# The inverse roots of the first token tiles: one VectorE step and GpSimd's power in place of ScalarE's root and VectorE's Newton steps

## The chip, the core and the metric

The kernel runs on one core of a Trainium2 chip. A core has five engines that run side by side and wait for each other through semaphores: TensorE (PE in the profile, with its weight loads shown as PEld), VectorE (DVE), ScalarE (ACT), GpSimd (POOL) and SyncE (SP), which here only issues DMA transfers. Each engine takes its own instructions strictly in the order in which they were written. Matmul results land in PSUM, everything else lives in SBUF.

The metric is the device time of one execution in microseconds (us). Smaller is better.

## The reference, cut to what matters

The input `x` holds 4 sequences of 1024 tokens with 512 features, that is, 4096 rows. `cond` has one row of 128 numbers per sequence.

```python
scale = cond @ norm_w.T + 1.0                        # one factor per sequence and feature
ms = jnp.mean(x * x, axis=-1, keepdims=True)         # one number per token
h = x * (scale[:, None, :] * jax.lax.rsqrt(ms + EPS))
u = h @ up_w.T                                       # 512 -> 4096
val, gate = jnp.split(u, 2, axis=-1)
h = val * jax.nn.gelu(gate, approximate=False)
hq = act_quant(h)                                    # 8 bits per token
wq = weight_quant(down_w)                            # -1, 0, 1
y = hq @ wq.T                                        # 2048 -> 512
return y + x
```

The change touches `rsqrt(ms + EPS)` alone, and that only for the first 512 tokens. For each token it is one number.

## The kernel before, in words

The kernel takes the four sequences one after the other. For a sequence it computes the up projection in 16 groups of columns, with gate and value beside each other, quantizes the result and multiplies it by the rounded down weights. From the second sequence on, the up and down products of neighbouring sequences are interleaved, and TensorE is never short of work. The first sequence has to begin from nothing. This beginning, the head, is what the change touches: about the first 20 us.

The order of the work is written out by hand (`tc.manual_schedule()`): every engine receives its instructions in the order of the Python text, so whatever stands ahead in an engine's queue is done first.

The head does this for the first 512 tokens, the tiles n = 0 to 3 of 128 tokens each:

- SyncE asks for tiles 0 and 1 in one transfer, 2 and 3 in a second, then for the first rows of the up weights, and so on. ScalarE's queue brings the row of `cond`.
- TensorE multiplies dummy tiles (`keep_warm`, L967) while it waits for data. These dummies stand in its queue like any other work: 4 of them ahead of the small matmul `pd` (L236), and 7 between `pd` and the first transposes.
- `first_sum` (L918) sums the squares of a tile: tiles 0 and 2 on ScalarE, 1 and 3 on VectorE. The sums go to the columns of `ssq0`.
- `rsqrt_root` (L925) lets ScalarE take the square root of two columns, and `rsqrt_steps` (L931) lets VectorE take the reciprocal of it and one Newton step: five short VectorE instructions. The result goes to two columns of `rs0`. This is done once for tiles 0 and 1, once for tiles 2 and 3.
- `cond_range_steps` (L214) makes the factor `dg` of the first sequence in four short VectorE instructions. The small matmul `pd`, and so all 7 dummies after it, wait for `dg`. In the kernel before, these four are interleaved with the first Newton steps by `in_turn` (L305). In the same way `w_factor_steps` (L293), the factor of the first weight tile (three instructions), is interleaved with the second Newton steps.
- `first_scale` (L945) multiplies a tile by its inverse roots: tiles 0, 1 and 2 on ScalarE, tile 3 on VectorE.
- `first_turn` (L952) transposes the scaled tile on TensorE, four 128x128 blocks per tile, into four PSUM banks `ptx`. Bank k holds block k of all four tiles. The tiles are turned in the order 0, 1, 3, 2. After them come the four transposes `pw` of the first weight tile (`w_turn`, L339), which GpSimd has scaled (`w_scale`, L331).
- `first_high` (L959, ScalarE) and `first_low` (L963, VectorE) split each bank into two 16-bit parts, `w_high` (L363) and `w_low` (L372) do it for the weights, and `plain_first` (L644) multiplies them. From there on TensorE is almost never idle.

Later tiles have their own way: `rsqrt` (L488 to L491) with one VectorE or GpSimd step for the mean and one GpSimd instruction `pow` with the exponents from `neghalf`. Tiles 4 to 7 go through it in `second_part` (L1040).

ScalarE works with a table of functions that is loaded by an instruction of its own. The kernel before loads the one with the square root at L904, while it waits for data, and the one with the nonlinearity (Gelu) at L1042, in the middle of `second_part`. Squares and copies run under either table.

GpSimd begins with two instructions MODIFY_POOL_CONFIG, which stand ahead of its first piece of work and name the code that it is to run. It meets such a pair again further on, where it changes between elementwise work and the maximum over partitions.

Of the kernel before, what the change touches and what calls it, by code (L numbers as in the profile page):

```python
# [2 lines left out]

# [6 lines left out]
F32 = mybir.dt.float32  # L10
# [4 lines left out]
AF = mybir.ActivationFunctionType  # L15
# [4 lines left out]
P = 128  # L20
# [31 lines left out]
def glu_quant_kernel(  # L52
# [158 lines left out]
        PE.transpose(pm, mx, ident)  # L211
        return pm

    def cond_range_steps(pm, b0, b1):  # L214
        n = b1 - b0
        dg = sm.tile([B, B], F32, name=f"dg_{b0}", tag="dg")[:n, :n]
        yield dg
        d4 = sm.tile([B, 1], F32, name=f"d4_{b0}", tag="d4")[:n]
        DVE.tensor_reduce(d4, pm, AX.X, ALU.max)
        yield  # L220
        DVE.tensor_scalar(d4, d4, 1e-30, None, ALU.max)
        yield
        pow2_floor(d4)
        yield
        DVE.tensor_scalar(dg, ident[:n, :n], d4, 1.0 / X_UP, ALU.mult, ALU.mult)

    def cond_range(pm, b0, b1):
        steps = cond_range_steps(pm, b0, b1)
        dg = next(steps)
        in_turn(steps)  # L230
        return dg

    def cond_spread(dg, b0, b1, tag):
# [53 lines left out]
    def w_largest(j, t0=0, t1=2):  # L287
        t = slice(t0, t1)
        am = sm.tile([P, 2], F32, name=f"wam_{j}_{t0}", tag="wam")[:, t]
        DVE.tensor_reduce(am, wn(j)[:, t], AX.X, ALU.max, apply_absolute_value=True)  # L290
        return am

    def w_factor_steps(j, am, t0=0, t1=2):  # L293
        t = slice(t0, t1)
        pow2_floor(am)
        yield
        DVE.scalar_tensor_tensor(
            sw[:, j, t], am, 2.0**-100, undo_up[:, t], ALU.max, ALU.mult
        )
        yield  # L300
        if j not in iv:
            iv[j] = sm.tile([P, 2], F32, name=f"iv_{j}", tag="iv", bufs=3)
        DVE.reciprocal(iv[j][:, t], sw[:, j, t])

    def in_turn(*steps):  # L305

        for _ in zip_longest(*steps):
            pass

    def w_factor(j, am, t0=0, t1=2):  # L310
        in_turn(w_factor_steps(j, am, t0, t1))

    def w_range(j, t0=0, t1=2):
        w_factor(j, w_largest(j, t0, t1), t0, t1)
# [582 lines left out]

    ctx.enter_context(tc.manual_schedule())
    start_t = sm.tile([P, 1], F32, name="start_t", bufs=1)
    eps = sm.tile([P, 1], F32, name="eps", bufs=1)  # L900
    DVE.memset(eps, EPS)
    ACT.dma_start(out=cn, in_=cond[0:1])
    SP.dma_start(out=nw, in_=norm_w.rearrange("(k p) c -> p k c", p=P))
    ACT.activation(start_t, one, AF.Sqrt)  # L904


    X0 = H[:, 4:8].rearrange("p s h d -> p (s h) d")
# [10 lines left out]
    def first_sum(n, eng=ACT):  # L918
        v, j, a = X0[:, n], junk[:, n % 4], ssq0[:, n : n + 1]
        if eng is ACT:  # L920
            ACT.activation(j, v, AF.Square, accum_out=a)
        else:
            eng.scalar_tensor_tensor(j, v, 1.0, v, ALU.mult, ALU.mult, accum_out=a)

    def rsqrt_root(n, m):  # L925

        z = sm.tile([P, m], F32, name=f"newton_{n}", bufs=1)
        ACT.activation(z, ssq0[:, n : n + m], AF.Sqrt, scale=1.0 / D, bias=eps)
        return z

    def rsqrt_steps(n, m, z):  # L931

        t, y = ssq0[:, n : n + m], rs0[:, n : n + m]
        ms = sm.tile([P, m], F32, name=f"mean_sq_{n}", bufs=1)
        DVE.reciprocal(y, z)
        yield
        DVE.tensor_scalar(ms, t, 1.0 / D, EPS, ALU.mult, ALU.add)
        yield
        DVE.tensor_tensor(z, y, y, ALU.mult)
        yield  # L940
        DVE.scalar_tensor_tensor(z, z, -0.5, ms, ALU.mult, ALU.mult)
        yield
        DVE.scalar_tensor_tensor(y, z, 1.5, y, ALU.add, ALU.mult)

    def first_scale(n, eng):  # L945
        r = rs0[:, n : n + 1]
        if eng is ACT:
            ACT.activation(X0[:, n], X0[:, n], AF.Copy, scale=r)
        else:
            eng.tensor_scalar(X0[:, n], X0[:, n], r, 1.0, ALU.mult, ALU.mult)  # L950
# [34 lines left out]
    pm = cond_over(mx, 0, 1, "A")  # L985
    first_sum(0)
    first_sum(1, DVE)
    root = rsqrt_root(0, 2)
    keep_warm(4)
    steps = cond_range_steps(pm, 0, 1)  # L990
    dg = next(steps)
    next(steps)
    next(steps)
    in_turn(rsqrt_steps(0, 2, root), steps)
    pd = cond_spread(dg, 0, 1, "A")
    keep_warm(7)
    first_sum(2)
    first_sum(3, DVE)
    am = w_largest(0, 1, 2)
    root = rsqrt_root(2, 2)  # L1000
    factor = w_factor_steps(0, am, 1, 2)
    in_turn(rsqrt_steps(2, 2, root), islice(factor, 2))
    first_scale(0, ACT)
    first_scale(1, ACT)
    in_turn(factor)
    first_scale(3, DVE)
    first_scale(2, ACT)
    w_scale(0, (1,))
    cond_undo(pd, 0, 1)
    ptx = [po_bank(f"ptx_0_{k}") for k in range(3)] + [bank("A", 2, name="ptx_0_3")]  # L1010
    for n in (0, 1, 3, 2):
        first_turn(n, ptx)
    w_turn(0, [bank("E", 2, name=f"pw_0_{t}") for t in (1, 0)], (1,))
    w_range(0, 0, 1)
# [16 lines left out]
    def second_part():  # L1031
        w_turn(0, ts=(0,))
        w_high(0, (0,))
        w_low(0, (0,))
        w_scale(1, (1,))
        first_sum(6)
        first_sum(7)
        first_low(0, 1, ptx[1])
        first_low(0, 2, ptx[2])
        rsqrt(ssq0[:, 4:8], rs0[:, 4:8], DVE)  # L1040
        first_low(0, 3, ptx[3])
        ACT.activation(start_t, neghalf[:, 0:1], AF.Gelu)  # L1042

# [546 lines left out]
```

## Time and profile before

| quantity | value |
|---|---|
| median of 3 runs | 727.5 us (727.32, 727.5, 730.2) |
| the profiled execution's own time | 727.02 us |
| its span in the profile | 725.2 us, so 1.8 us lie around it |
| TensorE busy | 718.7 us, 99% of the span |
| VectorE, ScalarE, GpSimd busy | 583.2, 396.4 and 195.9 us |
| ScalarE's table loads | L904 at 1.29 us, L1042 at 17.46 us, 1.28 us each |
| first work of GpSimd after four memsets | 10.59 us (L331) |

In a line of a timeline the first number is the start in us from the span's beginning, the second the duration; then come the engine, the line of the kernel, the operation, what is written and read with the shapes, and how many instructions were merged into the line. A bracket names the idle time of the engine just before and what ended it. In a chain of waits each line gives the start, the share of time and who held the end up in it. The chain for the whole span is 97% TensorE, so the time is the sum of what TensorE does and of the few places where it waits; nearly all of the latter lie in the head.

### The profile page before, as it was taken

Reading aid. Unit: us, or ns where it says so; the run is one execution under the profiler, and the core shown is the slowest. Engines: PE = TensorE matmul, PEld = TensorE weight load, DVE = VectorE, ACT = ScalarE, POOL = GpSimd, SP = SyncE. Lnnn points to the kernel's source line nnn. Section 1 sums busy time; section 2 is a strip of 40 time slices with the busy share of each in tenths; the row PEclk is TensorE's granted clock in tenths of the full one; section 3 lists DMA queues with packets and bytes.
Section 4 is the critical chain, followed back from the end, with each engine's and each line's share of the span. In section 5 each row is a group of like instructions: output and inputs, shape, how many; then the busy total and the mean of one; then the engine's idle time right before and its main releaser. Section 6 shows DMA issues by size and latency. Waiting matters only on the chain.

```text
span 725.2 us, 10130 instructions
## 1 busy us (share of the span) xinstructions
PE 718.7 (99%) x3656; PEld 358.4 (49%) x3656; DVE 583.2 (80%) x824; ACT 396.4 (55%) x622; POOL 195.9 (27%) x205
## 2 busy tenths in 40 slices
PE   8999999999999999999999999999999999999998
PEld 4544444444444446665444445665444444445844
DVE  8977887985698899787689897687678888755897
ACT  6769866772337674554335676544433665332274
POOL 1578796775100033340000030360020000000100
DMA  9399999989544565867745646766955455443253
GB/s 322 103 310 276 295 264 254 279 172 225 117 103 102 132 144 141 206 164 169 176 101 103 131 101 183 192 160 160 202 118 102 102 102 102 102 101 89 95 183 116
DMA packets 224062, 117.83 MB, mean 162 GB/s; under 512 B 186358, under 2 KB 196743, under 8 KB 224012
## 3 DMA queue, kind: packets, MB, share of 16 engines
q1 hardware_dynamic: 223722, 116.86, 65.7%
q8 instruction: 28, 0.46, 0.3%
q10 hardware_dynamic: 290, 0.33, 0.1%
q14 instruction: 22, 0.18, 0.1%
HBM read 49.50 MB, written 23.09 MB: 100 GB/s over the span
## 4 chain that ended last, share of the span: by engine, by line
PE 97%; DMA 2%; ACT 0%; DVE 0%; issue 0%; SPq 0%; ACTq 0%
PE A L586 34%; PE E L586 17%; PE pg L601 11%; PE pv L601 10%; PE B L586 9%; PE po L854 8%; PE po_end L806 4%; DMA SXY<-H 1%; PE po L806 1%; DMA H<-in_x_dram 1%; PE ptx L955 1%; PE pv L644 0%; PE po_B L854 0%; PE pg L644 0%; PE pw L339 0%; PE po_E L854 0%
## 5 line engine op out<-in xcount | busy, mean ns | idle before, releaser
L586 PEld LDWEIGHTS <-SXY 128*128 128x128 f16 x2016 | 197.2, 98 | 232.3 <-issue 0.6
L586 PE MATMUL A<-R,SXY 128*128 128x512 f16 x1152 | 266.3, 379 | 0.0
L586 PE MATMUL E<-R,SXY 128*128 128x512 f16 x576 | 140.0, 379 | 0.1
L684 DVE SCALAR_TENSOR_TENSOR H<-A,sg,t 128x512 f32<-128x512 f32 x48 | 36.0, 750 | 69.8 <-PE A L586 69.7
L736 POOL PARTITION_ALL_REDUCE am<-R x8 | 14.3, 1793 | 229.7 <-DVE R L722 229.7
L778 DVE TENSOR_TENSOR H<-H,am 128x1024 f32<-128x1024 f32 x64 | 76.2, 1216 | 0.0
L601 PEld LDWEIGHTS <-SXY 128*128 128x128 f16 x486 | 47.4, 98 | 58.0 <-DMA SXY<-H 0.9
L697 ACT ACTIVATE t<-t,sg 128x512 f32<-128x512 f32 x48 | 34.6, 721 | 66.7 <-DVE t L694 66.6
L586 PE MATMUL B<-R,SXY 128*128 128x512 f16 x288 | 70.0, 379 | 0.0
L720 DVE TENSOR_REDUCE gm<-H 128x512 f32<-128x1024 f32 x56 | 69.0, 1232 | 1.0
L601 PE MATMUL pg<-R,SXY 128*128 128x512 f16 x252 | 57.9, 379 | 0.4 <-DMA SXY<-H 0.4
L601 PE MATMUL pv<-R,SXY 128*128 128x512 f16 x234 | 54.4, 379 | 0.0
L681 ACT ACTIVATE t<-B,sg 128x512 f32<-128x512 f32 x48 | 33.0, 687 | 36.3 <-PE B L586 36.3
L490 POOL TENSOR_SCALAR ssq<-ssq 128x2 f32<-128x2 f32 x12 | 3.9, 322 | 172.4 <-ACT xt L520 123.2
L664 ACT COPY t<-A 128x512 f32<-128x512 f32 x48 | 27.9, 582 | 39.8 <-PE A L586 39.5
L854 PE MATMUL po<-wd,R 128*128 128x256 fp8e4 x384 | 48.5, 273 | 0.0
L786 ACT ACTIVATE H<-H 128x1024 f32<-128x1024 f32 x38 | 39.9, 1051 | 14.1 <-DVE H L778 11.3
L676 ACT COPY v<-E 128x512 f32<-128x512 f32 x48 | 28.1, 585 | 30.9 <-PE E L586 27.7
L854 PEld LDWEIGHTS <-R 128*128 128x128 bf16 (+1 forms) x416 | 40.7, 98 | 8.5
L703 DVE SCALAR_TENSOR_TENSOR H<-v,sg,t 128x512 f32<-128x512 f32 x48 | 37.9, 790 | 7.9 <-ACT t L697 7.9
L722 DVE TENSOR_TENSOR R<-R,gm 128x512 f32<-128x512 f32 x56 | 41.7, 745 | 1.3
L700 DVE TENSOR_TENSOR v<-A,v 128x512 f32<-128x512 f32 x48 | 32.8, 682 | 11.8 <-PE A L586 10.6
(202 smaller groups left out, 981.7 us busy)
## 6 DMA issues: line engine op xcount, KB each, us to landing
SXY<-s_dram SPq DMA_DIRECT2D x48, 256.0 KB, 3.0
s_dram<-SXY SPq DMA_DIRECT2D x18, 384.0 KB, 3.2
H<-in_L_cond_up_w_dram SPq DMA_DIRECT2D x13, 512.0 KB, 5.4
SXY<-s_dram SPq DMA_DIRECT2D x48, 128.0 KB, 3.1
xr<-in_x_dram SPq DMA_DIRECT2D x19, 256.0 KB, 3.0
out_dram<-xr SPq DMA_DIRECT2D x19, 256.0 KB, 2.4
H<-in_x_dram SPq DMA_DIRECT2D x8, 512.0 KB, 5.5
R<-in_L_cond_down_w_dram SPq DMA_DIRECT2D x8, 512.0 KB, 7.7
```

What stands on the lines that cost most here:

```text
L586: PE.matmul(o, s[:, w, k, :], tv[:, :, c, l, k, :], start=start and n == 0, stop=stop and n == len(TERMS) - 1, skip_group_check=True,)
L601: PE.matmul(ps, a[k // 2][:, w, k % 2, :], XP[:, l, k, h * TOK : (h + 1) * TOK], start=n == 0, stop=n == len(terms) - 1,)
L681: ACT.activation(cur["t1"], pb, AF.Gelu, scale=gain(g, 1))
L684: DVE.scalar_tensor_tensor(h_half(g - 1, 0), prev["A"], gain(g - 1, 0), prev["t1"], ALU.mult, ALU.mult)
L697: ACT.activation(prev["t2"], prev["t2"], AF.Gelu, scale=gain(g - 1, 1))
L703: DVE.scalar_tensor_tensor(h_half(g - 1, 1), prev["v"], gain(g - 1, 0), prev["t2"], ALU.mult, ALU.mult)
L720: DVE.tensor_reduce(gm[0], v, AX.X, ALU.max, apply_absolute_value=True)
L722: return [largest, lambda: DVE.tensor_tensor(m, m, gm[0], ALU.max)]
L778: DVE.tensor_tensor(v, v, r.to_broadcast([P, 2, TOK]), ALU.mult)
L786: ACT.activation(v, v, AF.Copy, bias=MAGIC)
L806: PE.matmul(po.rearrange("p (y c o) -> p y c o", c=2, o=P), q[:, a, h, j], wd8[:, :, j // n, j % n, :, y0:y1].rearrange("p c o y -> p y c o"),
L854: PE.matmul(po, w[:, j], m, start=start and j == 0, stop=stop and j == n - 1, skip_group_check=True,)
```

## The change

Six things change, all in the head:

- Both times, the square root and the five Newton instructions go. In their place stands `rsqrt`: one VectorE instruction for mean and epsilon, and one GpSimd `pow` over two columns. For tiles 0 and 1 it stands ahead of the factor `dg` in VectorE's queue, for tiles 2 and 3 ahead of the maximum over the weight tile.
- `cond_range` and `w_factor` run undivided again; nothing is interleaved.
- ScalarE's first table is the one with Gelu. The load in `second_part` and its trial instruction go.
- The order on ScalarE and VectorE around the scalings: ScalarE scales tiles 0, 1, 2, VectorE scales tile 3 after the whole factor of the weight tile.
- The tiles are turned in the order 0, 1, 2, 3.
- The constant `eps` and its memset go.

In the built programs the number of table loads falls from 2 to 1, VectorE has 9 instructions fewer, ScalarE 4 fewer (two roots, a table load and its trial), GpSimd 2 more. The two MODIFY_POOL_CONFIG now stand ahead of the first `pow`. TensorE's instructions are the same in kind, number and order but for the source of the third and fourth group of transposes. One transfer each for the down weights and `cond` uses another semaphore, so that the first down-weight transfer waits for tiles 4 and 5 to land instead of the second half of the first weight tile.

```diff
@@ cond_range, w_factor: generators with in_turn become plain functions
-    def cond_range_steps(pm, b0, b1):
+    def cond_range(pm, b0, b1):
...
-    def in_turn(*steps):
-
-        for _ in zip_longest(*steps):
-            pass
...
@@ the head
-    eps = sm.tile([P, 1], F32, name="eps", bufs=1)
-    DVE.memset(eps, EPS)
...
-    ACT.activation(start_t, one, AF.Sqrt)
+    ACT.activation(start_t, one, AF.Gelu)
...
-    def rsqrt_root(n, m):
-
-        z = sm.tile([P, m], F32, name=f"newton_{n}", bufs=1)
-        ACT.activation(z, ssq0[:, n : n + m], AF.Sqrt, scale=1.0 / D, bias=eps)
-        return z
-
-    def rsqrt_steps(n, m, z):
-
-        t, y = ssq0[:, n : n + m], rs0[:, n : n + m]
-        ms = sm.tile([P, m], F32, name=f"mean_sq_{n}", bufs=1)
-        DVE.reciprocal(y, z)
-        yield
-        DVE.tensor_scalar(ms, t, 1.0 / D, EPS, ALU.mult, ALU.add)
-        yield
-        DVE.tensor_tensor(z, y, y, ALU.mult)
-        yield
-        DVE.scalar_tensor_tensor(z, z, -0.5, ms, ALU.mult, ALU.mult)
-        yield
-        DVE.scalar_tensor_tensor(y, z, 1.5, y, ALU.add, ALU.mult)
...
     first_sum(0)
     first_sum(1, DVE)
-    root = rsqrt_root(0, 2)
+    rsqrt(ssq0[:, 0:2], rs0[:, 0:2], DVE)
     keep_warm(4)
-    steps = cond_range_steps(pm, 0, 1)
-    dg = next(steps)
-    next(steps)
-    next(steps)
-    in_turn(rsqrt_steps(0, 2, root), steps)
+    dg = cond_range(pm, 0, 1)
     pd = cond_spread(dg, 0, 1, "A")
     keep_warm(7)
     first_sum(2)
     first_sum(3, DVE)
+    rsqrt(ssq0[:, 2:4], rs0[:, 2:4], DVE)
     am = w_largest(0, 1, 2)
-    root = rsqrt_root(2, 2)
-    factor = w_factor_steps(0, am, 1, 2)
-    in_turn(rsqrt_steps(2, 2, root), islice(factor, 2))
+    w_factor(0, am, 1, 2)
     first_scale(0, ACT)
     first_scale(1, ACT)
-    in_turn(factor)
+    first_scale(2, ACT)
     first_scale(3, DVE)
-    first_scale(2, ACT)
     w_scale(0, (1,))
...
-    for n in (0, 1, 3, 2):
+    for n in (0, 1, 2, 3):
         first_turn(n, ptx)
...
         first_low(0, 3, ptx[3])
-        ACT.activation(start_t, neghalf[:, 0:1], AF.Gelu)
```

The function that both roots now call was there before, for later tiles:

```python
def rsqrt(ssq, rs, eng=POOL):
    eng.tensor_scalar(ssq, ssq, 1.0 / D, EPS, ALU.mult, ALU.add)
    POOL.tensor_tensor(rs, ssq, neghalf[:, : rs.shape[-1]], ALU.pow)
```

More of the change, by code (lines that the diff above doesn't have):

```diff
@@ L1 @@
 from contextlib import ExitStack
-from itertools import islice, zip_longest
 import concourse.bass as bass
@@ L212, in cond_over @@
         return pm
-    def cond_range_steps(pm, b0, b1):
+    def cond_range(pm, b0, b1):
         n = b1 - b0
-        dg = sm.tile([B, B], F32, name=f"dg_{b0}", tag="dg")[:n, :n]
-        yield dg
         d4 = sm.tile([B, 1], F32, name=f"d4_{b0}", tag="d4")[:n]
         DVE.tensor_reduce(d4, pm, AX.X, ALU.max)
-        yield
         DVE.tensor_scalar(d4, d4, 1e-30, None, ALU.max)
-        yield
         pow2_floor(d4)
-        yield
+        dg = sm.tile([B, B], F32, name=f"dg_{b0}", tag="dg")[:n, :n]
         DVE.tensor_scalar(dg, ident[:n, :n], d4, 1.0 / X_UP, ALU.mult, ALU.mult)
-    def cond_range(pm, b0, b1):
-        steps = cond_range_steps(pm, b0, b1)
-        dg = next(steps)
-        in_turn(steps)
         return dg
@@ L291, in w_largest, with w_factor @@
         return am
-    def w_factor_steps(j, am, t0=0, t1=2):
+    def w_factor(j, am, t0=0, t1=2):
         t = slice(t0, t1)
         pow2_floor(am)
-        yield
         DVE.scalar_tensor_tensor(
@@ L299, in w_factor_steps @@
         )
-        yield
         if j not in iv:
@@ L303, in w_factor_steps @@
         DVE.reciprocal(iv[j][:, t], sw[:, j, t])
-    def in_turn(*steps):
-        for _ in zip_longest(*steps):
-            pass
-    def w_factor(j, am, t0=0, t1=2):
-        in_turn(w_factor_steps(j, am, t0, t1))
     def w_range(j, t0=0, t1=2):
@@ L923, in first_sum @@
             eng.scalar_tensor_tensor(j, v, 1.0, v, ALU.mult, ALU.mult, accum_out=a)
-    def rsqrt_root(n, m):
-        z = sm.tile([P, m], F32, name=f"newton_{n}", bufs=1)
-        ACT.activation(z, ssq0[:, n : n + m], AF.Sqrt, scale=1.0 / D, bias=eps)
-        return z
-    def rsqrt_steps(n, m, z):
-        t, y = ssq0[:, n : n + m], rs0[:, n : n + m]
-        ms = sm.tile([P, m], F32, name=f"mean_sq_{n}", bufs=1)
-        DVE.reciprocal(y, z)
-        yield
-        DVE.tensor_scalar(ms, t, 1.0 / D, EPS, ALU.mult, ALU.add)
-        yield
-        DVE.tensor_tensor(z, y, y, ALU.mult)
-        yield
-        DVE.scalar_tensor_tensor(z, z, -0.5, ms, ALU.mult, ALU.mult)
-        yield
-        DVE.scalar_tensor_tensor(y, z, 1.5, y, ALU.add, ALU.mult)
     def first_scale(n, eng):
@@ L987, in glu_quant_kernel @@
     first_sum(1, DVE)
-    root = rsqrt_root(0, 2)
+    rsqrt(ssq0[:, 0:2], rs0[:, 0:2], DVE)
     keep_warm(4)
-    steps = cond_range_steps(pm, 0, 1)
-    dg = next(steps)
-    next(steps)
-    next(steps)
-    in_turn(rsqrt_steps(0, 2, root), steps)
+    dg = cond_range(pm, 0, 1)
     pd = cond_spread(dg, 0, 1, "A")
```

## The prediction

> **What bounds the kernel now.** I read the chain of waits over the whole span first. It is 97% TensorE, so a change in the head is worth only what it does to TensorE's start into steady work. Then I read the list of TensorE's waits:
>
> ```profile
> engine line waited for: us in total, times, longest us
> PE pz L971 <- DVE eps L901: 1.5, 1, 1.5
> PE pg L644 <- ACT SXY L363: 0.7, 1, 0.7
> PE pg L601 <- DMA SXY<-H: 0.4, 1, 0.4
> PE pd L236 <- DVE dg L225: 0.3, 1, 0.3
> PE pg L644 <- ACT R L959: 0.2, 1, 0.2
> ```
>
> All but one (0.4 us, at 48.8 us) lie before 14 us. From there TensorE runs through: whatever the first transposes gain or lose, the end gains or loses. So I asked for the chain of the stretch 6.3 to 13.9 us:
>
> ```profile
> 7.05 0.02 ACTq L928
> 7.07 0.05 issue
> 7.12 0.30 ACT newton L928
> ...
> 8.35 0.62 DVE R L923 x2
> ...
> 9.05 0.30 ACT newton L928
> 9.35 0.62 ACT H L948
> 9.97 0.05 issue
> 10.02 2.14 PE ptx L955 x16
> 12.16 0.45 PE pw L339 x4
> ```
>
> The second root on ScalarE, at 9.05, waits for VectorE's sum of tile 3, and the first scaling stands behind that root in ScalarE's queue, though its own factor was ready at 8.35. That is the stall that the change can remove. What comes next is read from TensorE's timeline (7.7 to 12.3 us):
>
> ```profile
> 7.95 0.38 PE L236 MATMUL pd<-dg,one 1*128 1x1 f32 x2 [0.33 <-DVE dg L225]
> 8.26 1.68 PE L971 MATMUL pz<-H 128*128 128x512 f16 x7
> 10.02 2.14 PE L955 MATMUL ptx<-ident,H 128*128 128x128 f32 x16
> ```
>
> The 7 dummies start at 8.26 and follow each other by 0.216 (single starts 8.70, 8.91, 9.13, 9.34, 9.56), so they free TensorE at 9.78 however early the scaling is. Only 0.24 us lies between that and 10.02. The dummies wait for `pd`, and `pd` for `dg`.
>
> Last, GpSimd's lines: when it works, what a `pow` costs, and how long after its MODIFY_POOL_CONFIG it works:
>
> ```profile
> 10.59 0.90 POOL L331 TENSOR_SCALAR H<-H,iv 128x512 f32<-128x512 f32 x1 [10.17 <-DVE iv L303]
> ```
>
> ```profile
> L331 POOLq MODIFY_POOL_CONFIG x2: 11/11/11, 0.8 to 0.8; - x2
> ```
>
> ```profile
> L491 POOL TENSOR_TENSOR rs<-ssq,neghalf x13: 700/707/1062, 18.6 to 481.5; 128x2 f32<-128x2 f32 x12, 128x4 f32<-128x4 f32 x1
> ```
>
> ```profile
> 178.28 0.38 POOL L729 PARTITION_ALL_REDUCE ready<-ready  x1 [5.91 <-issue]
> ```
>
> **The change part by part**, against the profiled execution (727.02 us; span 725.2 and 1.8 around it; 0.5 below the median 727.5).
>
> *First root.* VectorE's sum of tile 1 ends at 7.02, ScalarE's of tile 0 at 7.04. The one VectorE step (0.16, by its rows L937 and L490) runs 7.08 to 7.24. GpSimd answers 0.08 later (18.35 + 0.16 to 18.59 in the later use), so `pow` starts at 7.32. For two columns it takes 0.71 by the median of the 12 rows of that shape, 0.93 by the first of them in time (at 87.0 us), 1.06 by the four-column row, which is also its first call. I take 0.71, the same shape, and keep 1.06 for the range: done at 8.03, at worst 8.38.
>
> *ScalarE.* No root stands between its squares and its scalings. Tile 2's square ends at 8.39 as before (its data lands at 7.64). Scalings overlap by 0.09, so the first starts at 8.35 and three follow by 0.62: ends 9.05, 9.67, and the third if its factor is there. The first was 9.26 to 9.96 before: 0.9 us earlier.
>
> *The dummies.* The new VectorE step is now ahead of `dg`'s four instructions: the maximum starts at 7.16 instead of 6.94, and with its own 0.27 and three dependent steps of 0.2 (now without Newton steps between) `dg` ends at 8.01 instead of 7.89. `pd`, the dummies and the earliest transpose shift by the same 0.12: 9.90. That, not the scaling, is what ends last. So of ScalarE's 0.9 us, 0.12 us arrives.
>
> *Second root.* Behind `dg`, VectorE sums tile 3 from 7.92 (0.35 earlier than 8.27) to 8.61, the step ends at 8.80, `pow` runs 8.88 to 9.59, and ScalarE scales tile 2 from 9.65 to 10.35. TensorE asks for it after two tiles of four blocks at 0.109: 9.90 + 0.06 (the first block's longer spacing, 10.02 to 10.18) + 0.87 = 10.83. Slack 0.48. Tile 3 on VectorE: weight maximum 8.73 to 9.40, factor to 9.98, scaling to 10.43; wanted at 11.27. The factor at 9.98 instead of 10.48 lets GpSimd scale the weight tile by 10.98 (0.90 by its row), wanted by `pw` at 11.7; the two `pow` ahead of it in GpSimd's queue are done at 9.59.
>
> *Sum up to `pw`.* 16 blocks without the gap of 0.12 that stood before the second tile (10.40 to 10.63 instead of 0.11): `pw` starts at 9.90 + 0.06 + 16 x 0.109 = 11.70. Before it was 11.995. Gain 0.30: 0.12 from the start, 0.12 from the gap, 0.06 from the second long spacing that followed it.
>
> *After `pw`.* `first_high` 0, `w_high` and the other three run on ScalarE without a break from 12.63 to 14.96 and hold TensorE, so all of it moves by 0.30. The weight data for VectorE's L290 at 13.93 lands by 13.3; started at 13.63 it still finds it. The down-weight transfer issued later (after tiles 4 and 5 instead of at 8.98) is read first at 43.6 us by ScalarE's sums and hides behind 20 us of work; if that were gone it would cost its own delay of about 1.5. Tile 6 and 7's squares, read after 16 us, landed at 11.96.
>
> *Table load.* ScalarE saves 1.41 us (17.46 to 18.87) ahead of L363. But TensorE is busy from 16.0 on; its one stall there is 0.10 at 21.30, waiting for VectorE's L372 (20.57 to 21.25), and that stands behind the `pow` of tiles 4 to 7, not behind ScalarE. So 0; with 0.10 as the most. The Trainium skill ("ScalarE: Activation LUTs", What ACT_TABLE_LOAD costs) puts a switch at 1.28 us for the load and 1.38 for a drain, 2.66 together; this trace shows the 1.28, and the next cast 1.41 after the load began. By the page's figure 2.66 us of ScalarE would be freed, and the sum would still be 0.
>
> *`eps`.* One memset of 0.06 less (0.03 from start to start) in VectorE's queue. The first dummy, which the list of waits shows behind it, may start 0.03 earlier; `pd` waits for `dg` 6 us later and hides that.
>
> Sum: 727.02 - 0.30 = 726.7; on the median 727.5 - 0.3 = **727.2 us**, 0.04% less.
>
> **The unknown: GpSimd's readiness.** Before, GpSimd's first work after its MODIFY_POOL_CONFIG (0.83) is at 10.59, and there it answered 0.07 after its wait ended: by 10.5 it was ready, and the trace does not say since when. The change asks it at 7.32. The nearest rows are the three other starts after such a pair: 172.61 to 178.28, 321.78 to 328.07 and 489.80 to 496.00, that is 5.7 to 6.3 us with nothing to wait for. The DMA engines' share was 0.86 to 1.07 in those stretches, 0.46 and then 1.00 in the head, so neither easier nor harder. From 0.83 they give 6.5 to 7.1: ready 0.2 us before it is asked. I take that. The other end is 10.5. A start of `pow` at L puts the three scalings at L + 0.75, + 1.37 and + 1.98, TensorE's last tile at L + 3.18 and `pw` at L + 3.61. Up to L = 8.1 that hides behind the dummies; the break-even is 8.4; at 10.5 it is 14.1, a loss of 2.1, or 2.35 if the second `pow` takes 1.06.
>
> The Trainium skill ("GPSIMD Engine Reference", Instruction dispatch) speaks against the change here: the first call of newly loaded code pays about 6 us, 5.95 measured between the configuration and the first work. An estimate from that page: counted from 0.83, the code is in at 6.8, still hidden; counted from the call at 7.32, `pow` would start at 13.3 and the loss be 4.9, which the answer within 0.07 at 10.59 speaks against.
>
> **The rivals.**
> - *GpSimd's code arrives late.* One mechanism: `pow` starts when the code is in, not when its input is; ScalarE's scalings and then the transposes wait. For it: GpSimd has done nothing but memsets so far, and the margin is 0.2 us against a spread of 0.6. Against: the three rows. Slower from L = 8.4 on; halfway, L = 9.5, `pw` starts at 13.1 and the time is 728.6, at the end 729.6 to 729.9.
> - *The gain is eaten before TensorE.* The step ahead of `dg` costs 0.3 instead of 0.12 (if nothing overlaps), or tile 3's sum is stretched by GpSimd beside it as L950 was at 19.69 (0.96 instead of 0.49): then its end is 9.3, tile 2's scaling 11.1 and `pw` 12.0. Either way 727.4 to 727.5, nothing moves.
> - *All of ScalarE's 0.9 us arrives.* 726.6. Only if the dummies left the way, and the queue order excludes it unless `dg` also came earlier.
>
> **How the numbers follow.** Forecast 0.55, late code 0.25, eaten 0.17, all of it 0.03. The likeliest gives 727.2, on its own 726.8 to 727.5. Low end of the range: the largest gain (0.30 + 0.10 for the stall + 0.12 if `dg` is not delayed = 0.5) from the profiled 727.02, less 0.1: 726.4. High end: late code almost to its bound, 727.5 + 2.1 = 729.6, beyond which less than 1 in 10 is left. About 0.5% (3.6 us) is what a measurement of this kernel can tell from no change. None of the cases reaches it: same 0.94; slower 0.04 for a late start that costs TensorE more than the sum shows; faster 0.02.
>
> **What would show it.** Right: `pow` at 7.3 and 8.9, the first scaling at 8.35, transposes from 9.9 without a gap, `pw` at 11.7, no table load at 17.5, then the old order of times 0.3 earlier. Wrong: idle time of GpSimd behind its step ("issue" before the first `pow`), the first scaling after 9.2, transposes after 10.1. The sum fails most likely at the 0.2 us margin of GpSimd.

## The result and the profile after

The changed kernel takes **728.8 us** (median of 22 runs, 727.82 to 730.13). The kernel before, run beside it, takes 727.58 us (median of 22 runs). The ratio is 1.0015, with a 95% interval from 1.001 to 1.0021: the change costs 0.7 to 1.5 us where a gain of 0.3 us was forecast. The profiled execution of the changed kernel took 728.59 us, its span 726.8 us; before, the span was 725.2 us.

TensorE is still the bound (719.1 us busy against 718.7). So most of the 1.6 us between the two spans are waits, and the list of TensorE's waits of the changed kernel has them:

```profile
engine line waited for: us in total, times, longest us
PE pz L929 <- DVE ready L705: 1.5, 1, 1.5
PE pg L581 <- DMA SXY<-H: 1.1, 1, 1.1
PE pg L624 <- ACT SXY L343: 0.7, 1, 0.7
PE ptx L913 <- ACT H L906: 0.5, 1, 0.5
PE po L834 <- DVE xr L875: 0.5, 1, 0.5
PE pg L624 <- ACT R L917: 0.2, 1, 0.2
```

Four lines differ from before. The transposes `ptx` now wait 0.5 us for ScalarE's scaling; before, no wait of theirs was listed. The wait for the transfer into SXY has grown from 0.4 to 1.1 us. A wait for VectorE's `xr` is new. The wait of `pd` for `dg` (0.3) is no longer listed; in this execution the data of tiles 0 and 1 landed 0.54 us earlier than in the profile of before (5.75, 6.29 before). I matched TensorE's instructions of the two profiles one by one: the changed kernel is 0.27 us late when it leaves the head, 0.69 us more at 48.8 us and 0.65 us more at 318 us, which with small steps makes 1.57.

The first of these three losses is in the head. This is the chain of waits of the changed kernel from 6 to 18 us (start, share of time, who held the end up):

```profile
7.64 0.71 DVE R L901 x2
...
8.44 0.18 DVE ssq L470
8.62 0.01 issue
8.63 0.74 POOL rs L471
9.38 0.02 issue
9.40 0.73 ACT H L906
10.13 0.04 issue
10.17 2.32 PE ptx L913 x16
12.49 0.45 PE pw L319 x4
```

`pow` (L471) starts at 8.63, and everything behind it follows without a gap. The chain puts its start down to VectorE's step of 8.44, but that is the step of tiles 2 and 3. The input of the first `pow`, the step of tiles 0 and 1, was there at 6.75, since the data of these tiles had landed at 5.75. GpSimd let it wait 1.9 us. TensorE's timeline shows what the late scaling cost:

```profile
7.99 1.68 PE L929 MATMUL pz<-H 128*128 128x512 f16 x7
10.17 2.32 PE L913 MATMUL ptx<-ident,H 128*128 128x128 f32 x16 [0.50 <-ACT H L906]
12.33 0.60 PE L319 MATMUL pw<-ident,H 128*128 128x128 f32 x4
```

The dummies had left TensorE at 9.67, and it stood idle for 0.50 us. `pw` starts at 12.33; it was 11.995 before and 11.70 in the forecast.

### The profile page after: what moved, and what is told of

Its sections match the earlier page's. It is cut to its first block, busy times and chain, and to the rows that moved or that the text cites. A ratio compares the mean times of both kernels' runs of the same rounds, so it can differ in the third digit from the quotient of the medians.

```text
span 726.8 us, 10119 instructions
## 1 busy us (share of the span) xinstructions
PE 719.1 (99%) x3656; PEld 358.4 (49%) x3656; DVE 584.6 (80%) x815; ACT 394.4 (54%) x618; POOL 196.6 (27%) x207
## 4 chain that ended last, share of the span: by engine, by line
PE 95%; DMA 2%; DVE 1%; ACT 1%; POOL 0%; SPq 0%; issue 0%; DVEq 0%; POOLq 0%; ACTq 0%
PE A L566 34%; PE E L566 17%; PE pg L581 11%; PE pv L581 10%; PE B L566 9%; PE po L834 8%; PE po_end L786 4%; DMA SXY<-H 1%; PE po L786 1%; DMA H<-in_x_dram 1%; PE ptx L913 1%; PE pv L624 0%; PE po_B L834 0%; PE pg L624 0%; DVE nx L549 0%; POOL rs L471 0%
## 5 line engine op out<-in xcount | busy, mean ns | idle before, releaser
L834 PE MATMUL po<-wd,R 128*128 128x256 fp8e4 x384 | 48.5, 273 | 0.0
L834 PEld LDWEIGHTS <-R 128*128 128x128 bf16 (+1 forms) x416 | 40.7, 98 | 8.5
L702 DVE TENSOR_TENSOR R<-R,gm 128x512 f32<-128x512 f32 x56 | 43.4, 775 | 1.3
L683 DVE SCALAR_TENSOR_TENSOR H<-v,sg,t 128x512 f32<-128x512 f32 x48 | 37.7, 786 | 7.9 <-ACT t L677 7.9
```

What stands on the lines that cost most here:

```text
L683: DVE.scalar_tensor_tensor(h_half(g - 1, 1), prev["v"], gain(g - 1, 0), prev["t2"], ALU.mult, ALU.mult)
L702: return [largest, lambda: DVE.tensor_tensor(m, m, gm[0], ALU.max)]
L834: PE.matmul(po, w[:, j], m, start=start and j == 0, stop=stop and j == n - 1, skip_group_check=True,)
```

## The experiments

**Theory.** GpSimd's first code comes too late for the first `pow`. **Rivals.** The first `pow` really waits for VectorE's second step; TensorE is held up by something other than GpSimd; the loss lies behind the head. In every run the readings come from one profiled execution, the ratios from the timed runs.

### The changed kernel once more

The kernel is unaltered. It shows how far the start of the first `pow` moves from one execution to the next.

> The changed kernel once more, unaltered. Late code: the first power starts near 8.6 us, 1.3 or more after its input is ready, the transposes start near 10.2 and the weight transposes near 12.3, 0.3 later than before. That is a quarter of the 1.2 us measured. If the rest belongs to the change, TensorE's wait for the transposed weights near 49.7 is again about 1.1 us (0.4 before) and the wait for VectorE near 319 us is there again (0.5). If it is chance, these two differ from the first profile and only the head's 0.3 is the same.

Measured: 729.12 us against 727.82 before, ratio 1.0022 (1.0008 to 1.0036). The profiled execution took 734.0 us, and it is the theory writ large. GpSimd's and TensorE's timelines:

```profile
11.98 1.41 POOL L471 TENSOR_TENSOR rs<-ssq,neghalf 128x2 f32<-128x2 f32 x2 [11.55 <-issue]
13.38 0.69 POOL L311 TENSOR_SCALAR H<-H,iv 128x512 f32<-128x512 f32 x1
```

```profile
8.75 1.46 PE L929 MATMUL pz<-H 128*128 128x512 f16 x6
13.52 3.04 PE L913 MATMUL ptx<-ident,H 128*128 128x128 f32 x16 [3.31 <-ACT H L906]
16.36 1.06 PE L319 MATMUL pw<-ident,H 128*128 128x128 f32 x4
```

The input of `pow` was ready at 7.15, it ran at 11.98. The bracket now names "issue", so no other engine was late. TensorE was idle for 3.31 us, and then something was added that the forecast's formula lacks: from the eleventh transpose on the blocks follow each other by 0.213 instead of 0.109 us. By stretches (us; busy time and number of instructions of PE, PEld, DVE, ACT, POOL; granted TensorE clock; DMA share; GB/s):

```profile
13.50:14.50 1.00, 0.98 (x7) 0.79 (x8) 0.96 (x3) 1.00 (x2) 0.57 (x1) 1.00 1.04 393
14.50:17.40 2.90, 2.90 (x15) 2.32 (x13) 1.92 (x8) 0.88 (x2) 1.05 (x1) 0.58 1.04 412
17.40:20.00 2.60, 1.84 (x10) 0.89 (x10) 1.89 (x4) 2.55 (x5) 0.00 (x0) 0.81 0.89 350
```

The granted clock falls to 0.58 in the second stretch, behind the idle time, and recovers after some 3 us (the trace's own record has 0.5 from 14.95 to 18.36, so it fell only 1.4 us after TensorE had begun to work again); in the first profile of the changed kernel it was 1.00 in all these stretches. The Trainium skill ("TensorE: Matmul & The Clock Gate", Part 1: The HAM clock gate) says that about 3.4 us of idleness halve the clock; the row of 3.31 us idle and the doubled spacing agree with it.

### A small GpSimd instruction that waits for nothing

The kernel before, with one GpSimd instruction on a constant at the head of its queue. If it starts when the code is there, its start is the readiness.

```diff
+    probe = sm.tile([P, 1], F32, name="probe", bufs=1)
+    POOL.tensor_tensor(probe, one, one, ALU.pow)
```

> The kernel before with one small power (one column, inputs known from the start) as GpSimd's first instruction; nobody waits for it. It starts when GpSimd can first work. Late code: at 8.3 to 8.9 us. The prediction's premise: at 6.5 to 7.1 us, and then the power of the changed kernel waited for something else, such as the second VectorE step, which ended at 8.61 when it started at 8.63. Time: the same as before within 0.3 us, since GpSimd's next work is at 10.6.

> The probe of GpSimd's first possible start once more, with the transfers as they are: a second draw. If the start is a property of the run (code load beside the first data), it lies anywhere between 8.5 and 12.0 and not at the first draw's 8.75. If it is fixed, it is 8.7 to 8.8 again.

Measured: 728.06 us, ratio 1.0002 (0.9991 to 1.0013); a second execution took 727.01 us. GpSimd's timeline of the first and of the second profile:

```profile
8.75 0.59 POOL L901 TENSOR_TENSOR probe<-one 128x1 f32<-128x1 f32 x1 [8.33 <-DVE rs L945]
```

```profile
9.01 0.59 POOL L901 TENSOR_TENSOR probe<-one 128x1 f32<-128x1 f32 x1 [8.58 <-DVE R L925]
```

The constant was there before 1 us; the engines named in the brackets have nothing to do with it. So GpSimd was ready for its first work at 8.75 and 9.01 us, not at 6.5 to 7.1. That takes the ground from the rival that `pow` waits for VectorE's second step. Two later profiles of the changed kernel with other additions rule it out, since there the first `pow` starts before that step does: at 8.67 against 9.38 (six copies on ScalarE) and at 8.86 against 9.48 (nine memsets on VectorE).

### The same with the transfers held back

All of SyncE's transfers wait for that small instruction, so that the code loads while the DMA engines have almost nothing to do.

```diff
+    SP.dma_start(out=am_dram[0:1, 0:1], in_=probe[0:1, :])
     SP.dma_start(out=nw, in_=norm_w.rearrange("(k p) c -> p k c", p=P))
```

> The kernel before with the small power as GpSimd's first instruction and all of SyncE's transfers held back until it is done, so that GpSimd's code is loaded while the DMA engines have almost nothing else to do. If the code is late because it shares the DMA engines with the first data, the power starts well before the 8.6 to 12.0 seen so far, at 7.1 or earlier. If the load takes its own time, it starts in the same 8.6 to 12.0. The whole kernel is later by that start, 6 to 12 us; its time is of no interest.

Measured: 735.89 us in a single execution; the head starts late by construction. GpSimd's timeline:

```profile
8.46 0.59 POOL L901 TENSOR_TENSOR probe<-one 128x1 f32<-128x1 f32 x1 [8.03 <-issue]
```

Without the data transfers GpSimd is ready at 8.46, hardly earlier than 8.75 and 9.01 with them. Sharing the DMA engines with the first data is not what makes the first start later than 6.5 to 7.1. It comes 7.6 us after the configuration at 0.83. Beside the data it can be later still; whether the data are then the reason, a single execution without them can't tell. No row shows the load itself: from 0.83 to 8.46 the DMA records of this run hold two packets, those of the row of `cond`. What the runs show is that GpSimd starts nothing between its configuration and then; that the time goes into its code is the reading that fits, not something seen.

### Three dummies more

```diff
-    keep_warm(7)
+    keep_warm(10)
```

In the kernel before, to see what a later start of the transposes costs at the end.

> The kernel before with 10 dummies instead of 7 ahead of the first transposes: the dummies free TensorE at about 10.43 instead of 9.78, the gap ahead of the second tile is gone, and the weight transposes start 0.24 later (12.24). Nothing else of the head is touched. If a late start is passed on one to one, the time is 0.2 to 0.3 us above before. If the kernel turns a late start into more (the transfer that lands at 48.8, the alignment of VectorE and GpSimd near 318), it is about 1.2 us above, as with the change.

Measured: 727.41 us, ratio 0.9996 (0.9985 to 1.0008). It tells little: in the profiled execution tiles 0 and 1 landed at 5.73 instead of 6.29, so with three more dummies the transposes began at 10.21 (10.02 before) and `pw` at 11.96 (11.995). What it shows is that the landing of the first data moves by more than the effect that the forecast was about.

### Root for tiles 0 and 1, `pow` for tiles 2 and 3

```diff
     root = rsqrt_root(0, 2)      # kept, with its Newton steps
...
+    rsqrt(ssq0[:, 2:4], rs0[:, 2:4], DVE)
...
-    root = rsqrt_root(2, 2)
...
+    w_factor(0, am, 1, 2)
```

> The kernel before with the change for tiles 2 and 3 alone: tiles 0 and 1 keep the root and the Newton steps and the square-root table, tiles 2 and 3 take the power. Late code at 8.6 costs nothing here, as the second power is asked for at about 9.1: the first scaling starts at 8.35 instead of 9.26, the transposes at about 9.8 when the dummies end, the weight transposes at 11.6, 0.4 earlier, and the time is 0.4 us below before if passed on one to one. If the code comes after 9.5, the third scaling and with it the weight transposes are later and the gain is gone.

Measured: 728.23 us, ratio 1.0013 (1.0 to 1.0026). The first scaling starts at 8.23 and the transposes at 9.79, when the dummies let them: the forecast's reading that the dummies set the earliest start was right. But the `pow` of tiles 2 and 3, whose input was ready at 9.06, starts at 9.97, TensorE waits 0.7 us for the third tile and `pw` comes at 12.44. GpSimd is late even for the second pair.

### GpSimd taken out of the roots

The changed kernel, with VectorE's reciprocal in the place of `pow` for the first four tiles.

```diff
-    rsqrt(ssq0[:, 0:2], rs0[:, 0:2], DVE)
+    recip_v(0, 2)     # VectorE: mean and epsilon, then reciprocal
...
-    rsqrt(ssq0[:, 2:4], rs0[:, 2:4], DVE)
+    recip_v(2, 2)
```

> The changed kernel, but for the first four tiles VectorE's reciprocal stands where GpSimd's power stood. This leaves out the square root of these four tiles (the factor is 1/m instead of 1/sqrt(m)); all else is done. No scaling of the head waits for GpSimd's code any more; GpSimd's first work is the scaling of the weight tile, as before. Theory (GpSimd's first code load is the loss in the head, the head's mechanics are as forecast): first scaling at about 8.4, transposes from 9.8 to 10.0, pw at 11.7 to 11.9, so 0.4 to 0.6 us earlier there than in the changed kernel; the wait at 48.8 us stays near 1.0, and the time is 0.3 to 0.6 us below the changed kernel, 0.5 to 0.8 above before. Rival (the loss in the head is of another kind, such as the delayed dummies): transposes after 10.1 and the time as that of the changed kernel.

Measured: 728.83 us against 727.48 before, ratio 1.0022 (1.0014 to 1.0031). TensorE's timeline:

```profile
8.39 1.69 PE L934 MATMUL pz<-H 128*128 128x512 f16 x7
9.91 1.91 PE L918 MATMUL ptx<-ident,H 128*128 128x128 f32 x16
11.66 0.60 PE L319 MATMUL pw<-ident,H 128*128 128x128 f32 x4
```

Up to `pw` this is the forecast almost to the digit: transposes at 9.91 (forecast 9.90) without a gap, `pw` at 11.66 (11.70). So GpSimd's late start is what the changed kernel loses up to there. Behind `pw` not all of it arrives: the lead over the profile of before is 0.33 us at `pw` and 0.09 at 17 us, where TensorE's products wait for VectorE's L354. VectorE's timeline:

```profile
13.62 0.15 DVE L297 TENSOR_TENSOR sg<-sw,dx 128x2 f32<-128x2 f32 x1
13.85 1.22 DVE L280 TENSOR_REDUCE wam<-H 128x2 f32<-128x1024 f32 x1
```

L280 starts 0.08 us behind the end of the step ahead of it; in the profile of before (L290) it overlaps with that step by 0.09. So of 0.25 us that VectorE was early, 0.08 are left. The two kernels with reciprocals show this gap, no other profile does, and no row gives a reason for it.

The time is not lower either: the expected 0.3 to 0.6 us below the changed kernel did not come. The profiled execution took 727.80 us and was the second fastest of its twelve, so its profile doesn't show what the median one of 728.83 loses. That part stays open.

### VectorE's number of instructions

At 48.8 us TensorE waits for a transposing transfer that SyncE issues at about 41 us. In the profiles an instruction fetch of 8 KB falls 1.7 to 2.7 us after that issue with the kernel before and 5.1 us or more after it with the changed kernel (and with the one that has `pow` for tiles 2 and 3 alone). The idea is that such a fetch moves with the number of instructions that one engine has done. VectorE has 9 fewer, so nine one-column memsets were put into the changed kernel.

```diff
+    for _ in range(9):
+        DVE.memset(pad, 0.0)
```

> The changed kernel with 9 memsets of one column more on VectorE, where it waits for the first data, so that VectorE has as many instructions as before the change. Three runs with the power had TensorE wait 1.1 us for the transposed weights near 49.7 (8.7 from the transfer's issue to TensorE's start), three without it 0.3 to 0.4 (7.9 to 8.1); in the former a fetch of 8 KB of instructions falls 5 us behind that issue, in the latter 1.7 to 2.5. If that fetch delays the transfer and VectorE's count sets its time, the fetch comes at about 2 us again, the wait is 0.4 again and the time is 0.7 us below the changed kernel. If the wait has to do with the power or with the late head, it stays at 1.1. The first power starts between 8.6 and 12 either way.

Measured: 729.31 us against 727.92, ratio 1.0019 (1.001 to 1.0028). The fetch stays 5.15 us behind the issue, the wait at 0.9 us. This expectation missed: the fetch isn't VectorE's.

### ScalarE's number of instructions

The built program of ScalarE, counted with its semaphore instructions, is 6 shorter after the change, so six one-column copies were put behind its trial instruction, where it waits for data anyway.

```diff
     ACT.activation(start_t, one, AF.Gelu)
+    for _ in range(6):
+        ACT.activation(start_t, one, AF.Copy)
```

> The changed kernel with six one-column copies on ScalarE behind the trial instruction, where ScalarE waits for data; nothing is left out. The program of ScalarE then has as many instructions as before. Theory (the later instruction fetch at 46 us, which falls into the transposing transfer, is ScalarE's and goes by its count): the fetch is back at 1.7 to 2.5 us behind that transfer's issue, TensorE's wait for it at 48.8 us falls from about 1.0 to 0.3 to 0.6, and the time is 0.5 to 0.7 us below the changed kernel, 0.4 to 0.6 above before. Rival (the fetch is another engine's, or the wait has another cause): fetch at +5, wait 0.9 to 1.1, time as the changed kernel, 1.1 to 1.3 above before.

Measured: 728.25 us against 727.48, ratio 1.0008 (1.0 to 1.0017). The fetch is back at 2.3 us behind the issue and the wait is down from 1.1 to 0.6:

```profile
PE ptx L915 <- ACT H L908: 1.0, 1, 1.0
PE pg L624 <- ACT SXY L343: 0.7, 1, 0.7
PE pg L581 <- DMA SXY<-H: 0.6, 1, 0.6
PE pv L581 <- DVE H L609: 0.5, 1, 0.5
```

Over all the profiles of this study, the seven with the late fetch wait 0.6 to 1.2 us there (median 1.08), the eleven with the early one 0.3 to 0.8 (median 0.56). That the fetch is ScalarE's is shown, since its position follows ScalarE's count: in the eleven profiles with the early one ScalarE's program has 883 instructions, in the seven with the late one 877 to 881. That it costs about 0.5 us is likely, though the reciprocal kernel (late fetch, 0.6) doesn't fit, and single executions overlap. The same profile holds one more piece of evidence on `pow`: it starts at 8.67, while tiles 2 and 3 land only at 8.55, so VectorE's second step was not even begun. And it runs for 1.19 instead of 0.71 us, beside VectorE's sum of a tile (1.10 us in the run with the nine memsets, likewise).

### Both repairs together

The reciprocal and four copies (with the reciprocal, four bring ScalarE back to its former number).

> Both at once: the reciprocal in place of the power for the first four tiles (which leaves out their square root), and copies on ScalarE, four here, which bring its program to the same number of instructions as before. If both theories hold, and these two are the whole loss, the time is 0.9 to 1.3 us below the changed kernel, that is from 0.2 below to 0.2 above before, with pw at 11.7 to 11.9 and a wait of 0.3 to 0.6 at 48.8 us. If it stays 0.5 or more above before, a further part of the loss is elsewhere, first of all the wait for VectorE at 318 us.

Measured: 728.05 us, ratio 1.0006 (0.9997 to 1.0015), with `pw` at 12.05, the wait at 48.8 us at 0.5, the wait for `xr` still there:

```profile
PE pg L581 <- DMA SXY<-H: 0.5, 1, 0.5
PE po L834 <- DVE xr L875: 0.5, 1, 0.5
```

The median is 0.6 us above before, so a further part of the loss is elsewhere; the wait for `xr`, which the expectation named first, is in the list. The four kernels side by side: as changed 1.0015 and 1.0022, reciprocal 1.0022, copies 1.0008, both 1.0006. The copies are worth 0.5 to 1.2 us by these ratios, 0.8 by the medians of the two kernels with reciprocals. The reciprocal is worth nothing that these runs resolve, although it takes 0.7 us off `pw` in the profiles; the intervals are 0.6 us wide to either side.

### Root without Newton steps

The kernel before with the Newton steps left out (eight one-column memsets on VectorE stand in for them) and ScalarE's second root put behind its first scaling, so that this scaling doesn't wait for tile 3's sum, and GpSimd isn't needed either.

```diff
         DVE.reciprocal(y, z)
         yield
-        DVE.tensor_scalar(ms, t, 1.0 / D, EPS, ALU.mult, ALU.add)
...
     first_scale(0, ACT)
+    root = rsqrt_root(2, 2)
```

> The kernel before without the Newton steps (it leaves out that refinement of the inverse roots: each is the reciprocal of ScalarE's root alone), with ScalarE's second root behind the first scaling, and 8 memsets of one column to keep VectorE's count. Nothing waits for GpSimd before its weight scaling. The first scaling starts at 8.35, the transposes when the dummies end at 9.8, without gaps, and the weight transposes at 11.6, 0.4 earlier than before, if GpSimd's code is in by 10.7; TensorE's wait near 48.8 stays at 0.4. Time: 0.4 us below before, if the prediction's account of TensorE's start holds once the power is out of it.

Measured: 727.89 us against 727.92, ratio 1.0001 (0.9992 to 1.0011). The gain of 0.4 us didn't show. In the profile tiles 2 and 3 landed at 8.51 (7.64 before), and the square of tile 2 stands ahead of the first scaling in ScalarE's queue; `pw` came at 12.08: the data was the bound, not the roots. So even a faster root that needs no GpSimd brings nothing measurable here.

### The wait at 318 us

Why does VectorE come late with `xr`? In VectorE's timelines of before and after (the same steps under their two line numbers) the lateness grows in two jumps:

```profile
304.09 0.77 DVE L703 SCALAR_TENSOR_TENSOR H<-v,sg,t 128x512 f32<-128x512 f32 x1
304.78 1.21 DVE L722 TENSOR_TENSOR R<-R,gm 128x512 f32<-128x512 f32 x1
...
314.04 0.68 DVE L722 TENSOR_TENSOR R<-R,gm 128x512 f32<-128x512 f32 x1
314.64 1.75 DVE L833 TENSOR_TENSOR H<-R 128x1024 bf16<-128x1024 bf16 x1
```

```profile
300.70 0.69 DVE L813 TENSOR_TENSOR H<-R 128x1024 bf16<-128x1024 bf16 x1 [0.75 <-DMA R<-H]
...
305.47 1.01 DVE L683 SCALAR_TENSOR_TENSOR H<-v,sg,t 128x512 f32<-128x512 f32 x1
306.40 1.21 DVE L702 TENSOR_TENSOR R<-R,gm 128x512 f32<-128x512 f32 x1
...
315.64 1.76 DVE L702 TENSOR_TENSOR R<-R,gm 128x512 f32<-128x512 f32 x1
317.32 1.75 DVE L813 TENSOR_TENSOR H<-R 128x1024 bf16<-128x1024 bf16 x1
```

VectorE waits 0.75 us for L813, because a transposing transfer (292.48 to 299.04 before, 293.31 to 300.68 after) took 7.4 instead of 6.6 us. Shifted against GpSimd, its step L683 takes 1.01 instead of 0.77, and later L702 takes 1.76 instead of 0.68. GpSimd's step beside it, before and after:

```profile
314.41 3.11 POOL L533 TENSOR_TENSOR H<-H,sc 128x512 f32<-128x512 f32 x2 [2.18 <-ACT H L532]
```

```profile
315.35 3.18 POOL L513 TENSOR_TENSOR H<-H,sc 128x512 f32<-128x512 f32 x2 [1.79 <-ACT H L512]
```

Before, VectorE's step (314.04) starts 0.37 us ahead of GpSimd's; after (315.64), 0.29 us behind it. The twelve profiles up to here, the one with held-back transfers left out, show a threshold: measured against TensorE, VectorE's step at 301.6 was at most 0.15 us later than in the profile of before in the five without the wait, and 0.21 to 0.52 us later in the seven with it. In the five VectorE's step starts 0.26 to 0.38 us ahead of GpSimd's and takes 0.68 or 0.69 us, in the seven 0.29 to 0.32 us behind it and takes 1.75 or 1.76. All six profiles of the changed kernel and its variants have the wait, and one of the six of the kernel before and its variants (the small GpSimd instruction). The Trainium skill ("SBUF — State Buffer", SBUF: two separate sides) says that VectorE with two operands from SBUF and GpSimd lock a shared port for a whole instruction, whichever starts first; L702 has two such operands, and its 0.68 and 1.76 us agree.

Three kernels move that transfer in SyncE's queue behind the two loads of `x` rows that followed it: in the changed kernel, in the kernel before, and in the changed kernel with the six copies.

```diff
-                (None, p0, (..., (10, "x"), (10, "z"))),
+                (None, p0, (..., (10, "x"), (11, "x"))),
```

> The changed kernel with one transposing transfer (the third sequence's first tokens, and the fourth's) moved in SyncE's queue from ahead of two loads of x rows to behind them; nothing is left out. Theory for the wait of 0.5 us at 318 us: these loads stand behind the transposing transfer in the queue, land some tenths later in some executions, and VectorE, which waits for them at about 300 us, then falls 0.7 and again 1.1 us behind beside GpSimd's work. With the loads issued some 5 us earlier VectorE does not wait for them, the wait at 318 us goes, and the time is 0.4 to 0.7 us below the changed kernel, 0.4 to 0.8 above before. Rival: VectorE falls behind for another reason, the wait at 318 us stays and the time is that of the changed kernel. Second rival: the moved transfer now delays the loads behind it, TensorE waits there, and the time is above the changed kernel.

> The kernel before with the same transfer moved; nothing is left out. Theory: the profile of before has no wait at 318 us, but that of the same kernel with the small GpSimd instruction had it once in two, so the median falls by 0.1 to 0.4 us, to 727.1 to 727.4, and no timed run of the lower half is changed. Rival: the profiled execution stands for all, and nothing moves (within 0.1 us). Second rival, as above: TensorE waits for what stands behind the moved transfer, and the time is above before.

> The changed kernel with the transfer moved and the six one-column copies on ScalarE; nothing is left out. If both repairs add up, what is left of the loss is the head alone: 0.3 us by the two profiles, so 727.7 to 728.0, 0.2 to 0.5 above before. If it stays 0.8 or more above before, the head costs more in the timed runs than in the profiled ones, through late code of GpSimd in some of them.

Measured against 728.01 before: 731.47 (1.0052, 1.004 to 1.0065), 729.06 (1.0014, 1.0005 to 1.0023) and 731.32 us (1.0051, 1.0039 to 1.0064). All three slower. I had the wrong transfer: in the changed kernel VectorE's L813 waits for the transposing transfer itself, and more so when that comes later. VectorE's timeline and TensorE's waits in the first of the three:

```profile
303.13 1.59 DVE L813 TENSOR_TENSOR H<-R 128x1024 bf16<-128x1024 bf16 x1 [3.44 <-DMA R<-H]
```

```profile
PE po L834 <- DVE xr L875: 2.6, 3, 1.6
```

The miss answers the question all the same: 3.4 instead of 0.75 us of lateness at L813 makes 2.6 instead of 0.5 us of waiting for `xr`. VectorE's lateness at 300 us is passed on to TensorE, and the end of this transfer is one thing that sets it. The loads of the `x` rows can be another: with the nine memsets L813 is on time, and the 0.21 us arise at the two steps behind it, which wait for these loads.

The last two kernels issue the transfer earlier, at 285 to 286 us, which changes the computation: it overwrites quantized values that the products L834 have yet to read.

```diff
-                (None, p0, (..., (10, "x"), (10, "z"))),
+                (None, p0, (..., (10, "x"), (10, "y"))),
```

> The changed kernel with the same transposing transfer (the third and the fourth sequence's first tokens) issued earlier than in the changed kernel, as soon as its tokens are split, at about 284 us instead of 293; nothing is left out. Theory: VectorE's step L813 at about 300 us waits for the end of this transfer, which e12 has shown by delaying it; issued earlier, it is long done, VectorE's steps behind L813 start at least 0.3 us earlier than in the changed kernel, the wait at 318 us goes, and the time is 0.4 to 0.7 us below the changed kernel. Rival: the transfer now stands ahead of the spilled sums that TensorE needs next, and TensorE waits for these: time above the changed kernel. Second rival: VectorE waits for something else at 300 us (the two loads of x rows), and nothing moves.

> The kernel before with the same transfer issued earlier; nothing is left out. Theory: the executions of before that have the wait at 318 us lose it, the median falls by 0.1 to 0.5 us against before. Rivals as for the other: time above before by a new wait, or nothing moves (within 0.1 us).

Measured: 743.05 us (1.0204, 1.019 to 1.0218) and 741.07 us (1.0178, 1.0164 to 1.0192) against 728.16. TensorE waits 9.3 us in two places for the transfer, since its products share the part of R that it writes:

```profile
PE po L834 <- DMA R<-H: 9.3, 2, 5.2
```

That is 9.3 of the 13 to 15 us lost. Around the ends of these two waits (5.2 and 4.1 us) the granted clock was 0.5 as well, for 6.8 and 3.4 us (from 291.46 and 468.95 in the first of the two runs). TensorE comes out of the two places 8.1 and 5.7 us later against the profile of before, so the clock adds some 4 to 5 us to the waits. The wait for `xr` isn't listed in either, as the theory had it, but with TensorE late by 8 us that says little. Why the transfer took 0.8 us longer in the changed kernel isn't settled. In five of the seven profiles with the wait for `xr` an instruction fetch falls within 0.25 us of its issue, in none of the five without it; but two (the small GpSimd instruction and the nine memsets) wait without such a fetch near.

## Why the prediction was wrong

The forecast was 727.2 us, the result 728.8: inside the stated range (726.4 to 729.6) and inside "same", but on the other side of before. The forecast also held that nothing under 0.5% could be told from no change; with 22 runs each the interval, 0.1 to 0.21% slower, is clear of it.

- **The step that failed: "The unknown: GpSimd's readiness".** It took three later starts, 5.7 to 6.3 us behind their MODIFY_POOL_CONFIG, for the price of the first one, and came to 6.5 to 7.1 us. Measured, GpSimd is ready at 8.46 with idle DMA engines, in the others at 8.59 to 9.01 (seven profiles), 9.55, 9.97 and 11.98. The three rows were real, but a later start is another case than the first; why, no run shows. The reason given for their use, that the DMA engines were as busy there, was beside the point, as the run with held-back transfers shows. The rule of the Trainium skill that the prediction quoted ("GPSIMD Engine Reference", Instruction dispatch), about 6 us for the first call, agrees with the three later rows here and not with the first: 7.6 to 11.1.
- **The rival "GpSimd's code arrives late" is what happened.** Its formula held: the first scaling was put at L + 0.75 and came at L + 0.77 and L + 0.76 (8.63 to 9.40, 11.98 to 12.74); `pw` was put at L + 3.61 and came at L + 3.70 for L = 8.63. It failed at the late end, L = 11.98, by 0.8 us, through the halved clock. Its halfway price of 728.6 us lies near the result, but in part by accident, as the next point shows.
- **A second error: "After `pw`" moved everything rigidly.** With the reciprocals, 0.33 us gained at `pw` became 0.09 within the head. The head of the profiled execution of the changed kernel loses 0.3 us only. The wait for the transfer at 48.8 us (0.7 more) and the one for `xr` at 318 us (0.5) stood in no case of the forecast. Over the seven profiles with `pow` in the head, `pw` starts at 12.83 by the median, over the seven with roots that don't need GpSimd at 11.99 (left out: the held-back transfers, `pow` for tiles 2 and 3 alone, and the two with reciprocals). So 0.8 for the head, 0.5 for ScalarE's fetch and up to 0.5 at 318 us: more than the 1.1 measured. A fourth wait comes on top in five of the seven profiles with `pow` in the head and in no other: 0.2 to 0.5 us near 162 us (167 where the head was latest) for VectorE's L609. With the six copies TensorE comes out of it 0.9 us later against the profile of before. Each of these was seen in profiles; how the 1.1 divides, the timed runs don't resolve, and the reciprocals, which take GpSimd out, are no faster by their median. That part of the cause stays open.
- **"The dummies" was right:** they set the first transpose at 9.79 with `pow` for tiles 2 and 3 alone, and at 9.91 with the reciprocals, forecast 9.90. The 0.01 is luck in part: the reciprocals' data landed 0.29 us earlier than in the profile of before, and VectorE has a reciprocal more ahead of `dg`. Of 0.9 us on ScalarE only some tenths could have arrived.
- **"First root" was right on the price:** `pow` took 0.68 to 0.73 us where no sum of VectorE ran beside it, forecast 0.71; where one did, the first took 1.10 and 1.19.
- **"Table load" was right.** The load in `second_part` is gone and ScalarE stands idle instead:

```profile
18.70 0.58 ACT L343 CAST SXY<-pw 128x512 f16<-128x512 f32 x1 [0.93 <-PE pw L319]
```

  With the load, its trial and the two roots gone, ScalarE's program is six instructions shorter, and that had a price that the forecast left out: the fetch moved, for some 0.5 us at 48.8 us.

## What to carry to other kernels

The first work of GpSimd in a kernel is not priced by its later starts behind the same instructions: put a tiny instruction without inputs at the head of its queue and read when it starts. Don't put an engine into the first chain of a kernel because its operation is cheap; here 0.7 us of work waited 0.9 to 4.8 us for GpSimd to be ready. An effect of some tenths of a microsecond is smaller than what moves by itself from one execution to the next, such as the landing of the first data and waits that hang on a threshold far behind the change, so the profile of a single execution can't confirm it.

## What was unexpected of the hardware

- The first work of GpSimd starts no earlier than 7.6 us after its MODIFY_POOL_CONFIG with idle DMA engines and up to 11.1 us after it beside the first data; the three later ones took 5.7 to 6.3.
- 3.3 us of idle TensorE cost 0.8 us more up to `pw`: the granted clock fell to 0.58 between 14.5 and 17.4 us, and transposes came every 0.213 us instead of 0.109.
- The place of an 8 KB instruction fetch moved by 3 us when one engine's program became six instructions shorter, and back when they were put in again; the transposing transfer that it falls into was read 0.5 us later by the median of the profiles.
- The first two transfers of `x` land anywhere from 5.5 to 7.0 and from 7.1 to 8.8 us, with nothing changed ahead of them in their queue.
- VectorE's L702 takes 0.68 us where it starts 0.3 us ahead of a GpSimd step that reads SBUF, and 1.76 us where it starts 0.3 us behind it. That makes a threshold: 0.15 us of lateness at 301 us costs nothing, 0.21 costs 0.5 us at 318 us.
